# The experts' Gelu in half pieces, each followed by an exponential that nobody reads

## The chip, the cores and the metric

The kernel runs on one core of a Trainium2 chip. The metric is the device time of one execution in microseconds (us). A core has five engines that run side by side, each through its own queue in order: TensorE (PE, with its weight loads as PEld), VectorE (DVE), ScalarE (ACT), GpSimd (POOL) and SyncE (SP), which here only issues DMA transfers.

## The reference

The input is x, 4 sequences of 2048 tokens of 512 columns. Everything is in 32-bit floats.

```
xn  = layernorm(x)
qkv = xn @ qkv_w.T + qkv_b                      # 16 heads of 32 columns
att = softmax(q k^T * 32**-0.5) v               # per sequence and head, 2048 x 2048
a   = att @ proj_w.T + proj_b
idx = top_2(xn[:, 0, :] @ Wr + br)              # 2 of 8 experts for each sequence
h   = gelu(xn @ W1[idx] + b1[idx])              # the exact Gelu, 512 columns
f   = sum over the two experts of (h @ W2[idx] + b2[idx]) / 2
out = x + a + f
```

## The kernel before

**Units.** The work of attention is cut into 1024 units. A unit U is one sequence (4), one group of four heads (4), one chunk of 512 queries (4) and one tile of 128 keys (16 per chunk). For a unit, PE forms four score tiles of 128 keys x 512 queries (`shift`, line 725, writes minus the row maxima into the bank; `score`, line 733, adds the scores), and ACT takes their exponentials into one buffer `p` (line 849, four instructions of 512 columns). In the same turn of the loop PE forms four score tiles the other way round for a unit 22 turns ahead (`score_max`, line 715), whose maxima DVE takes (line 855). In each even unit, PE multiplies the last two `p` buffers with v (`weigh`, line 745, tile `acc`), and DVE adds that to a running sum. POOL adds the `p` buffers of a chunk up, one per unit (line 766; the last of a chunk is added by a DMA that POOL issues, line 764). There are four `p` buffers.

All PE results go to a ring of eight banks of 512 columns (`bank`, tag "bank"): each new tile takes the bank that was used longest ago, and has to wait until what was in it has been read. An even unit takes four banks for scores, four for the maxima's scores, and a ninth tile, `acc`.

**Dense products.** The other matrix products (q, k and v, the experts' two layers, the output projection) are laid into the odd units, one item each: 16 matmuls per item, most of them, which take PE 3.64 us. The class `Plan` decides which item goes into which odd unit. Some slots are fixed; the rest is filled in order. Every sixteenth slot (`s % NT == 5`) may be left empty, when the plan has slots to spare:

```python
if s in rests:
    owed += share
    if owed > 0 and not curve:
        owed -= 1
        continue
```

`curve` (line 147) keeps a slot from being left empty when the item just before it makes an activation due in it.

**The experts' layers.** The first layer (`w1` items) handles two chunks of 512 tokens at a time for one expert. It uses a scheme of seven half-size products (numbers 1 to 7 of `GAPS`) instead of eight, which `combine` adds up, on DVE, in two buffers `hT[0]` and `hT[1]`, one per chunk of tokens, each 128 x 4 column tiles x 512. A product comes in two halves q = 0, 1; half q fills the column tiles 2q and 2q+1. The eight items of one such block are, in order: 1 (q = 0), 1 (q = 1), 6, 7, 5 and 3 (q = 0), 5 and 3 (q = 1), 4, 2. So `hT[1]` has its first two column tiles after (3, 0), all four after (3, 1), and `hT[0]` is complete after (2, 1). There are 16 blocks (4 sequences, 2 pairs of chunks, 2 experts), and so 32 buffers to activate. After them come the second layer's items (`w2`), four for `hT[1]` (odd chunk) and then four for `hT[0]`.

**The activation.** `dense` puts a finished buffer under the number of a later unit, the next odd one:

```python
if (i, q) in ((3, 1), (2, 1)):
    at = U + 2 if U > 0 or U == -1 else U + 1
    curves[at] = hT[i == 3]
```

and the main loop issues the Gelu in that unit, right behind its four exponentials (lines 849 to 853). ACT computes a function from a table; where the next function isn't in the loaded table, the compiled program has an ACT_TABLE_LOAD ahead of it. The trace shows one ahead of each Gelu and one ahead of the first exponential after it. Other instructions on ACT that may stand between them are a normalisation of a token tile (`normal`, line 441), a copy (lines 524, 784), and three times a Sqrt (`root`, line 434).

The order on every engine is that in which the program issues (a manual schedule); waits between engines are derived from what each instruction reads and writes.

Of the kernel before, what the change touches and what calls it, by code (L numbers as in the profile page):

```python
# [9 lines left out]
F32 = mybir.dt.float32  # L10
BF16 = mybir.dt.bfloat16
U32 = mybir.dt.uint32
AF = mybir.ActivationFunctionType
# [4 lines left out]
P = 128  # L18
# [19 lines left out]
class Plan:  # L38
# [6 lines left out]
    def __init__(self, B, DC, NCH, NT, TPC):  # L45
# [13 lines left out]
        for G in range(1, B * DC):  # L59
            b, g = divmod(G, DC)  # L60
            first = (G - 1) * self.per_group
            for n, products in enumerate(GAPS):
                at = (11, 12, 13, 14, 15, 16, 17, 19) if g else (5, 6, 7, 8, 9, 11, 12, 13)
                fixed[first + 2 * at[n] + 1] = ("qk", b, g, products)
            if g == 0:
                at = [n for n in range(14, 32) if n % 8 != 2]
# [10 lines left out]
        for b in range(1, B):  # L77
            q1 = (b - 1) * self.per_seq + self.per_group
            q2 = q1 + self.per_group
            for k in range(TOP_K):  # L80
                at = q1 + ((NT - 1, q2 - q1 + 5 * NT - 1) if b > 1 else (-1, NT - 1))[k]
# [4 lines left out]
            for n in range(NT):  # L86
                self.extra.setdefault(q1 + 2 * (16 + n) + 1, []).append(("stats", b, n))
                c, i = divmod(n, TPC)
                at = q2 + 2 * (1 + 18 * (c // 2) + 5 * (c % 2) + i) + 1
# [3 lines left out]
            for p in range(NCH // 2):  # L93
                at = q2 + 2 * NT * (p + 1) - 1
# [46 lines left out]
        current, before, owed = [], None, 0  # L141
        for s in slots:
            if s in fixed:
                self.items[s] = [fixed.pop(s)]
                before = None
                continue
            curve = before is not None and before[0] == "w1" and before[4][-1] in ((3, 1), (2, 1))
            before = None
            if s in rests:
                owed += share  # L150
# [3 lines that stand above are left out]
            if not current:  # L154
                for queue in (proj, ffn):
                    if queue and queue[0][0] <= s:
                        current = queue.pop(0)[1]
                        break
            if current:
                before = current.pop(0)  # L160
                self.items[s] = [before]
# [77 lines left out]
def block_kernel(  # L239
# [16 lines left out]
    nc = tc.nc  # L256
# [12 lines left out]
    const = ctx.enter_context(tc.tile_pool(name="const", bufs=1))  # L269
# [7 lines left out]
    def bank(name):  # L277
        return ps.tile([P, CH], F32, tag="bank", name=name)
# [106 lines left out]
    nc.vector.tensor_copy(ident_b, ident)  # L385
    ones = const.tile([P, HD], F32, name="ones")
    nc.gpsimd.memset(ones, 1.0)
    ones_b = const.tile([P, P], BF16, name="ones_b")
    nc.gpsimd.memset(ones_b, 1.0)

# [90 lines left out]
    def product(pp, terms, last=True, first=True):  # L481

        for n, (lhsT, rhs) in enumerate(terms):
            for j in range(GH):
                nc.tensor.matmul(  # L485
                    pp[rows_of(j), :], lhsT[:, rows_of(j)], rhs,
                    start=(first and n == 0), stop=(last and n == len(terms) - 1),
                )

    kT, qT = {}, {}  # L490
    hT, bias, b1s = {}, {}, {}
# [16 lines left out]
    def project_v(b, n, xn, w, U):  # L508

        c, i = divmod(n, TPC)  # L510
        pp = bank(f"vps_{b}_{n}")
        product(pp, [(xn[:, d, ts(i, P)], w[:, d, :]) for d in range(DC)])
        t = pair.tile([P, D], F32, tag="vrow", name=f"v_{b}_{n}")
        nc.vector.tensor_tensor(t, pp, bv_bc, ALU.add)
        later(U + 2, lambda: nc.sync.dma_start(v_dram[b, c][:, i, :], t))

    def combine(i, x, c, b1, b2, on_dve):

        add = nc.vector.tensor_tensor
        biased = nc.vector.scalar_tensor_tensor  # L520
        if i == 1 and on_dve:
            nc.vector.tensor_copy(c[0, 0], x)
        elif i == 1:
            nc.scalar.activation(c[0, 0], x, AF.Identity)  # L524
        elif i == 6:
            add(c[0, 1], x, c[0, 0], ALU.add)
        elif i == 7:
            add(c[1, 0], x, c[0, 1], ALU.add)
        elif i == 5:
            biased(c[1, 1], x, b2, c[1, 0], ALU.add, ALU.add)  # L530
            add(c[0, 1], x, c[0, 1], ALU.add)
        else:
            at, b_ = {3: ((0, 1), b1), 4: ((1, 0), b2), 2: ((0, 0), b1)}[i]
            biased(c[at], x, b_, c[at], ALU.add, ALU.add)
# [29 lines left out]
    def blocks(kind, b, n, U):  # L564
# [10 lines left out]
        else:  # L575
# [4 lines left out]
            if n == 3:  # L580
                later(U + (2 if b == 0 else 4), lambda: nc.sync.dma_start(ws_dram[b, k], raw))

    outs = {}

    def dense(item, U, on_dve, between):
        kind, b = item[:2]
        tiles = [held[n] for n in plan.needs(item)]
        if kind == "qk":
            g, products = item[2:]
            for n, (i, p) in enumerate(products):  # L590
                wt, xt = tiles[2 * n : 2 * n + 2]
                pp = bank(f"qkps_{b}_{g}_{i}_{p}")
                product(pp, [(wt[:, d, 0, :], xt[:, d, :]) for d in range(2)])
                o = outs.setdefault((b, g, p), {})
                where = {1: (0, 0), 6: (0, 1), 7: (1, 0), 5: (1, 1)}.get(i)
                if where is not None:
                    c = 2 * p + where[1]
                    t = "kq"[where[0]]
                    o[where] = (kT if t == "k" else qT)[b, g, c] = kv_pool.tile(
                        [P, CH], F32, tag=t, name=f"{t}T_{b}_{g}_{c}",  # L600
                        bufs=2 * NCH if t == "k" else NCH + 3,
                    )
                combine(i, pp, o, bqkv[:, DC + g : DC + g + 1], bqkv[:, g : g + 1], on_dve)
                if n == 0:
                    between()
        elif kind == "v":
            n = item[2]
            project_v(b, n, tiles[1] if b else stage[0, n // TPC], tiles[0], U)
        elif kind == "w1":
            p, k, products = item[2:]  # L610
            for n, (i, q) in enumerate(products):
                wt, xt = tiles[2 * n : 2 * n + 2]
                if (i, q) in ((1, 0), (6, 0)):
                    cc = int(i == 6)
                    hT[cc] = stream.tile(
                        [P, DC, CH], F32, tag="h", name=f"h_{b}_{p}_{k}_{cc}", bufs=2
                    )
                pp = bank(f"hps_{b}_{p}_{k}_{i}_{q}")
                product(pp, [(wt[:, d, q, :], xt[:, d, :]) for d in range(2)])
                o = {(r, cc): hT[cc][:, 2 * q + r, :] for r in range(2) for cc in hT}  # L620
                cols = [b1s[b, k][:, 2 * q + r : 2 * q + r + 1] for r in range(2)]
                combine(i, pp, o, *cols, on_dve)
                if n == 0:
                    between()
                if (i, q) in ((3, 1), (2, 1)):
                    at = U + 2 if U > 0 or U == -1 else U + 1
                    curves[at] = hT[i == 3]
        elif kind == "w2":
            p, c, k, i = item[2:]
            w, row = tiles  # L630
            pp = bank(f"ops_{b}_{c}_{k}_{i}")
            product(pp, [(hT[c % 2][:, f, ts(i, P)], w[:, f, :]) for f in range(DC)])
            nc.vector.scalar_tensor_tensor(row, pp, 0.5, row, ALU.mult, ALU.add)  # L633
            later(U + 2, lambda: nc.sync.dma_start(part_dram[b, c, i], row))
        else:
            qc, i = item[2:]
            at, w, row = tiles
            pp = bank(f"prps_{b}_{qc}_{i}")
            product(pp, [(at[:, g, ts(i, P)], w[:, g, :]) for g in range(DC)])
            finish(b, qc, i, pp, row, U)  # L640

    def finish(b, qc, i, pp, row, U):
        tok = qc * CH + i * P
        nc.vector.tensor_tensor(row, pp, row, ALU.add)  # L644
        later(U + 2, lambda: nc.sync.dma_start(out[b, tok : tok + P, :], row))
# [15 lines left out]
    def sum_bias(t, other, pb):  # L661
        nc.gpsimd.tensor_tensor(t, t, other, ALU.add)
        nc.gpsimd.tensor_scalar(t, t, 0.5, None, ALU.mult)
        nc.gpsimd.tensor_tensor(t, t, pb, ALU.add)


    mv, sd, nb = stat_tiles(0)
# [27 lines left out]
    def place(u):  # L695
        rest, kt = divmod(u, NT)
        rest, qc = divmod(rest, NCH)
        return (*divmod(rest, DC), qc, kt)

    mx, negm, sacc, psums, sums, pT = {}, {}, {}, {}, {}, {}  # L700
    curves, waiting, ends = {}, {}, []

    def later(u, do):
        waiting.setdefault(u, []).append(do)
# [124 lines left out]
    for U in range(-LEAD, plan.units):  # L829
# [20 lines left out]
        curve = curves.pop(U, None)  # L850
        if curve is not None:
            flat = curve.rearrange("p f n -> p (f n)")
            nc.scalar.activation(flat, flat, AF.Gelu)
        for dst, t in maxima:
            nc.vector.tensor_reduce(dst, t, AX.X, ALU.max, negate=True)  # L855
        last = U + LEAD
# [7 lines left out]
        before = place(U - NT)[:3] if U >= NT else None  # L864
# [30 lines left out]
        for step, sb, n in plan.extra.get(U, []):  # L895
# [10 lines left out]
            else:  # L906
                c, i = divmod(n, TPC)
# [36 lines left out]
    U = plan.units  # L944
# [18 lines left out]
    for i in range(TPC):  # L963
        q = ts(i, P)
# [52 lines left out]
```

## Time and profile before

| | |
|---|---|
| median of 3 runs | 5042.79 us (5037.69 to 5044.59) |
| the profiled execution | 5042.55 us |
| its span, first to last instruction | 5040.8 us |
| mean granted TensorE clock | 0.997 |
| PE busy | 4947.0 us, 98% |
| POOL busy | 4429.2 us, 88% |
| DVE busy | 3740.2 us, 74% |
| ACT busy | 2394.0 us, 47% |
| ACT_TABLE_LOAD | 71, of 1.283 us each |
| Gelu, 128 x 2048 | 32, of 1.912 us each |

How to read the profile's rows: a group has its line, engine and operation, what it writes and reads with the shapes, how often; then the busy time in us and the mean of one in ns; then the idle time of the engine just before these instructions and what ended most of it. In a row of time the first two numbers are start and duration in us, and the brackets hold the idle time before and what ended it. "A <- B: 37.0, 35, 1.6" says that A waited for B 37.0 us in total, 35 times, 1.6 us at the longest.

### The profile page before, as it was taken

Reading aid. Unit: us, or ns where it says so; the run is one execution under the profiler, and the core shown is the slowest. Engines: PE = TensorE matmul, PEld = TensorE weight load, DVE = VectorE, ACT = ScalarE, POOL = GpSimd, SP = SyncE. Lnnn points to the kernel's source line nnn. Section 1 sums busy time; section 2 is a strip of 40 time slices with the busy share of each in tenths; the row PEclk is TensorE's granted clock in tenths of the full one; section 3 lists DMA queues with packets and bytes.
Section 4 is the critical chain, followed back from the end, with each engine's and each line's share of the span. In section 5 each row is a group of like instructions: output and inputs, shape, how many; then the busy total and the mean of one; then the engine's idle time right before and its main releaser. Section 6 shows DMA issues by size and latency. Waiting matters only on the chain. (4 is left out here: it accounts for less than half of the span.)

```text
span 5040.8 us, 107883 instructions
## 1 busy us (share of the span) xinstructions
PE 4947.0 (98%) x45028; PEld 1725.8 (34%) x45028; DVE 3740.2 (74%) x5909; ACT 2394.0 (47%) x4406; POOL 4429.2 (88%) x1498
## 2 busy tenths in 40 slices
PE   8999999999999999999999999999999999999998
PEld 2333333333333333333333333333333333333332
DVE  5777887777777788777777777877777777777762
ACT  1445445454444545454444444555444445454453
POOL 2799998999898998999889998999988988999981
PEclk9999999999999999999999999999999999999999
DMA  6333334433233434434224234434423343323312
GB/s 219 111 103 117 115 96 127 142 122 109 80 107 104 126 107 122 140 114 141 89 86 125 85 121 118 146 122 136 134 70 106 100 123 101 101 80 101 107 62 95
DMA packets 297128, 568.16 MB, mean 113 GB/s; under 512 B 24636, under 2 KB 144188, under 8 KB 279744
## 3 DMA queue, kind: packets, MB, share of 16 engines
q1 hardware_dynamic: 287568, 495.19, 29.4%
q0 software_dynamic: 9072, 66.06, 6.7%
q8 instruction: 354, 5.80, 0.5%
q14 instruction: 134, 1.10, 0.1%
HBM read 367.44 MB, written 127.66 MB: 98 GB/s over the span
## 5 line engine op out<-in xcount | busy, mean ns | idle before, releaser
L766 POOL TENSOR_TENSOR psum<-psum,p 128x2048 f32<-128x2048 f32 x819 | 3722.4, 4545 | 167.6 <-ACT p L849 129.2
L849 ACT ACTIVATE p<-s 128x512 f32<-128x512 f32 x4096 | 2118.0, 603 | 2364.9 <-PE m L715 2181.8
L855 DVE TENSOR_REDUCE mx<-m 128x1 f32<-128x512 f32 x4096 | 2544.2, 684 | 570.1 <-PE m L715 569.8
L733 PE MATMUL s<-qT,kT 32*128 32x512 f32 x8192 | 1919.1, 588 | 0.0
L715 PE MATMUL m<-kT,qT 32*128 32x512 f32 x8192 | 1911.3, 590 | 6.4 <-ACT h L524 3.4
L715 PEld LDWEIGHTS m<-kT,qT 32*128 32x128 f32 x8192 | 920.9, 184 | 334.9 <-issue 244.7
L745 PE MATMUL acc<-p,v 128*32 128x512 f32 x8192 | 988.5, 600 | 37.0 <-ACT p L849 37.0
L733 PEld LDWEIGHTS s<-qT,kT 32*128 32x128 f32 x8192 | 768.6, 185 | 29.2 <-issue 7.3
L485 PE MATMUL ops<-wb_w,h 128*32 128x512 f32 x4096 | 466.0, 595 | 0.6 <-ACT p L849 0.2
L745 PEld LDWEIGHTS acc<-p,v 128*32 128x32 f32 x8192 | 214.2, 109 | 737.0 <-ACT p L849 420.5
L762 POOL TENSOR_TENSOR psum<-p,p 128x2048 f32<-128x2048 f32 x63 | 287.5, 4563 | 203.2 <-ACT p L849 203.2
L754 DVE TENSOR_TENSOR sacc<-acc,sacc 128x512 f32<-128x512 f32 x448 | 309.9, 692 | 158.3 <-PE acc L745 158.3
L485 PE MATMUL hps<-xt,wt_w 128*32 128x512 f32 x3584 | 411.0, 596 | 2.5 <-ACT p L849 2.0
L725 PE MATMUL s<-negm,ones_b 32*128 32x512 bf16 x4096 | 405.7, 385 | 6.2 <-ACT p L849 5.9
L485 PE MATMUL qkps<-xt,wt_qk 128*32 128x512 f32 x3360 | 387.8, 599 | 9.8 <-ACT p L849 9.2
L725 PEld LDWEIGHTS <-ones_b 32*128 32x128 bf16 x4096 | 103.2, 91 | 858.2 <-issue 858.1
L870 DVE RECIPROCAL sums<-sums 128x128 f32<-128x128 f32 x252 | 237.6, 943 | 0.7 <-ACT sums L784 0.7
L485 PEld LDWEIGHTS ops<-wb_w,h 128*32 128x32 f32 x4096 | 120.0, 109 | 308.6 <-issue 229.8
L633 DVE SCALAR_TENSOR_TENSOR row<-ops,row 128x512 f32<-128x512 f32 x128 | 88.4, 691 | 170.3 <-PE ops L485 116.3
L485 PE MATMUL prps<-wb_proj,xl_at 128*32 128x512 f32 x1792 | 203.9, 595 | 0.3
L485 PEld LDWEIGHTS hps<-xt,wt_w 128*32 128x32 f32 x3584 | 103.3, 109 | 268.2 <-issue 186.1
L485 PEld LDWEIGHTS qkps<-xt,wt_qk 128*32 128x32 f32 x3360 | 97.3, 110 | 273.9 <-issue 181.6
(123 smaller groups left out, 1981.6 us busy)
## 6 DMA issues: line engine op xcount, KB each, us to landing
xt<-t_dram SPq DMA_DIRECT2D x181, 512.0 KB, 4.3
xt<-xn_dram SPq DMA_DIRECT2D x133, 512.0 KB, 5.0
psum<-p POOLq DMA_DIRECT2D x63, 1024.0 KB, 8.2
part_dram<-row SPq DMA_DIRECT2D x128, 256.0 KB, 2.0
v_dram<-v SPq DMA_DIRECT2D x64, 256.0 KB, 2.7
wt_w<-ws_dram SPq DMA_DIRECT2D x128, 128.0 KB, 3.3
v<-v_dram SPq DMA_DIRECT2D x64, 256.0 KB, 4.9
row<-in_x_dram SPq DMA_DIRECT2D x64, 256.0 KB, 6.5
```

Of the source, the lines that this page charges most:

```text
L485: nc.tensor.matmul(pp[rows_of(j), :], lhsT[:, rows_of(j)], rhs, start=(first and n == 0), stop=(last and n == len(terms) - 1),)
L633: nc.vector.scalar_tensor_tensor(row, pp, 0.5, row, ALU.mult, ALU.add)
L715: nc.tensor.matmul(t, qT[b, g, qc][r, ts(i, P)], kT[b, g, kc][r, :], start=True, stop=True)
L725: nc.tensor.matmul(tiles[j], ones_b[r, :], negm[b, g, qc][r, :], start=True, stop=False)
L733: nc.tensor.matmul(tiles[j], kT[b, g, kt // TPC][r, ts(kt % TPC, P)], qT[b, g, qc][r, :], start=False, stop=True,)
L745: nc.tensor.matmul(acc[r, :], held["v", (b, g, kt // TPC)][:, (kt + n) % TPC, r], pT[u + n][:, j, :], start=(n == 0), stop=(n == 1),)
L754: nc.vector.tensor_tensor(t, acc, t, ALU.add)
L762: nc.gpsimd.tensor_tensor(psums[b, g, qc], pT[u - 1], pT[u], ALU.add)
L766: nc.gpsimd.tensor_tensor(psums[b, g, qc], psums[b, g, qc], pT[u], ALU.add)
L849: nc.scalar.activation(pT[U][:, j, :], tiles[j], AF.Exp, scale=SCALE)
L855: nc.vector.tensor_reduce(dst, t, AX.X, ALU.max, negate=True)
L870: nc.vector.reciprocal(sums[before][:, q], sums[before][:, q])
```

## The change

The Gelu is done on two column tiles (128 x 1024) at a time. For `hT[1]` the two pieces follow the items with (3, 0) and (3, 1); for `hT[0]` both follow (2, 1), in the next odd unit and in the one after that. Directly behind each piece ACT computes an exponential of one column of a constant, into a tile that nothing reads. The plan's condition for a slot that must not be left empty is extended to the new units: after the item with (3, 0), and after the first `w2` item of an odd chunk.

```diff
@@ class Plan
-            curve = before is not None and before[0] == "w1" and before[4][-1] in ((3, 1), (2, 1))
+            curve = before is not None and (
+                before[0] == "w1" and before[4][-1] in ((3, 0), (3, 1), (2, 1))
+                or before[0] == "w2" and before[3] % 2 == 1 and before[5] == 0
+            )
@@ constants
+    unused = const.tile([P, 1], F32, name="unused")
@@ helpers
+    def following(U):
+
+        return U + 2 if U >= -1 else U + 1
...
+    def back_to_exp():
+
+        nc.scalar.activation(unused, ones[:, :1], AF.Exp)
@@ def dense, w1
-                if (i, q) in ((3, 1), (2, 1)):
-                    at = U + 2 if U > 0 or U == -1 else U + 1
-                    curves[at] = hT[i == 3]
+                if i == 3:
+                    curves[following(U)] = hT[1][:, 2 * q : 2 * q + 2, :]
+                if (i, q) == (2, 1):
+                    curves[following(U)] = hT[0][:, :2, :]
+                    curves[following(following(U))] = hT[0][:, 2:, :]
@@ main loop
         if curve is not None:
             flat = curve.rearrange("p f n -> p (f n)")
             nc.scalar.activation(flat, flat, AF.Gelu)
+            back_to_exp()
```

## The prediction

> **What bounds the kernel now.** I read first the page's shares of busy time, then who kept TensorE (PE) waiting, then ScalarE's (ACT's) groups by shape, then the order of time around one Gelu on ACT and on PE.
>
> ```profile
> PE 4947.0 (98%) x45028; PEld 1725.8 (34%) x45028; DVE 3740.2 (74%) x5909; ACT 2394.0 (47%) x4406; POOL 4429.2 (88%) x1498
> ```
>
> PE is busy 98% of the span of 5040.8 us, so only 94 us of PE idle can be won. ACT has half its time free; POOL (GpSimd) at 88% is the next limit. The waits of PE, longest first (total us, times, longest):
>
> ```profile
> PE acc L745 <- ACT p L849: 37.0, 35, 1.6
> PE qkps L485 <- ACT p L849: 9.2, 5, 4.7
> PE xt L455 <- ACT x L441: 6.0, 1, 6.0
> ```
>
> The first row is the only large one. In the order of time 31 of those waits, nearly all of 1.16 us, follow a Gelu directly. ACT's groups by shape:
>
> ```profile
> L849 ACT ACTIVATE p<-s 128x512 f32<-128x512 f32 x4096 | 2118.0, 603 | 2364.9 <-PE m L715 2181.8 <-issue 74.2 <-PE s L733 60.8
> L853 ACT ACTIVATE h<-h 128x2048 f32<-128x2048 f32 x32 | 61.2, 1912 | 0.4
> L849 ACT ACT_TABLE_LOAD x35 | 44.9, 1283 | 25.6 <-PE m L715 25.5
> L853 ACT ACT_TABLE_LOAD x32 | 41.1, 1283 | 0.6
> L441 ACT ACTIVATE xl_normal<-xl_normal,nb,sd 128x512 f32<-128x512 f32 x48 | 39.8, 829 | 0.0
> L434 ACT ACTIVATE sd<-sd 128x16 f32<-128x16 f32 x3 | 0.6, 215 | 7.5 <-DVE sd L433 7.5
> ```
>
> The load ahead of a Gelu starts at once (0.6 us idle over 32). The load back to Exp sits behind the wait of the next exponential: before its 35 instances ACT was idle 25.6 us, for scores (PE m). So 1.283 us of load starts only when the scores are ready. One Gelu on ACT in order of time (start, duration):
>
> ```profile
> 1718.64 2.07 ACT L849 ACTIVATE p<-s 128x512 f32<-128x512 f32 x4 [2.09 <-PE m L715]
> 1720.72 1.28 ACT L853 ACT_TABLE_LOAD   x1
> 1722.02 1.91 ACT L853 ACTIVATE h<-h 128x2048 f32<-128x2048 f32 x1
> 1724.24 1.28 ACT L849 ACT_TABLE_LOAD   x1 [0.31 <-PE m L715]
> 1725.53 2.07 ACT L849 ACTIVATE p<-s 128x512 f32<-128x512 f32 x4
> ```
>
> And PE beside it:
>
> ```profile
> 1718.82 0.59 PE L733 MATMUL s<-qT,kT 32*128 32x512 f32 x2
> 1719.34 3.64 PE L485 MATMUL hps<-xt,wt_w 128*32 128x512 f32 x32
> ...
> 1724.43 0.59 PE L733 MATMUL s<-qT,kT 32*128 32x512 f32 x2
> 1726.18 1.92 PE L745 MATMUL acc<-p,v 128*32 128x512 f32 x16 [1.16 <-ACT p L849]
> ```
>
> Undisturbed, PE goes on 0.52 us after the start of its last score matmul; here it took 1.75. That is **1.23 us lost** for a load that made the exponentials 1.28 late; so PE has 0.05 us of slack. The reason is in the code: in an even unit `acc` is the ninth tile of a ring of eight banks, so it takes the bank of the first score tile, which the first exponential frees.
>
> **What the losses before add up to.** I took, for all 32 Gelus, the time from the end of the four exponentials ahead to the start of those behind (4.82 here), and to the point where the scores were ready (3.53 here). 30 lose about 1.23: 36.9. One, at 2210 us, also has a 0.80 us normalisation (L441) on ACT between, with nothing extra on PE: 1.64. One, at 1980 us, also has the Sqrt with its own load, and the exponentials come at 6.22 instead of 3.53: 2.64. Sum **41.2 us**.
>
> **The change, part by part.** (1) *Half Gelus.* The two ACT rows of 512 and 2048 columns give (1912-603)/1536 = 0.852 ns a column, so 1024 columns are 603+436 = 1.04 us, or with the overhead taken from the 0.21 us of the tiny Sqrt 1.06. I take 1.05: 64 of them are 67 us of ACT instead of 61. (2) *64 more loads and 64 one-column exponentials.* The dummy has no wait: its operand is a constant, its target is nobody's. So its load starts when the half Gelu ends. The dummy takes 0.21, the row of the tiny Sqrt (0.215). Loads before: 32+35+4 = 71. After: 64+64+4+4 = 136. (3) *The chain in one piece.* From the end of the exponentials: 0.02 + load 1.283 + 0.015 + Gelu 1.05 + 0.02 + load 1.283 + 0.015 puts the dummy's start at 3.69. Adjacent exponentials overlap by 0.12 (four of 0.603 in 2.07), so the next real one can start between 3.78 and 3.90. I take 3.80, nearer the row of adjacent exponentials. Scores are ready at 3.53: late 0.27, less the slack of 0.05: **0.22 us lost a piece**, bounds 0.15 and 0.35. (For an undivided Gelu with the dummy the same sum is 4.65, late 1.12: nearly all of the 1.28 would stay. The halves are what makes the eager load fit.)
>
> (4) *Where the 64 pieces fall.* By the plan's rule every piece sits in an odd unit with a dense product of 3.64 us on PE: the product hides 3.53 us of ACT. Without a product, exponentials come 3.9 us apart and the window is 1.83; the price would be 2 us. The planner's new condition keeps the empty slots off these units: working the slots through by hand, three (units 53, 661, 901) move sixteen units on, and the products between move up. Same work, hence 0, with 2 us either way for what collides. Of the 64 pieces 45 meet nothing else: 45 x 0.22 = 9.9. Nine have PE transposes in their unit (of the maxima, or of a token tile), which widen the window to about 3.97: 0. Nine share the unit with a normalisation, which adds 0.80-0.10: chain 4.50, against scores ready at 4.13 (five, as the rows below show), 3.97 (two) and 3.53 (two): 5 x 0.32 + 2 x 0.48 + 2 x 0.92 = 4.4. One meets the Sqrt: 6.22-0.86+1.283+0.25 = 6.89, lost 3.3. Sum after: **17.6**.
>
> ```profile
> 847.55 1.28 ACT L853 ACT_TABLE_LOAD   x1
> 848.85 1.91 ACT L853 ACTIVATE h<-h 128x2048 f32<-128x2048 f32 x1
> 850.66 0.80 ACT L441 ACTIVATE xl_normal<-xl_normal,nb,sd 128x512 f32<-128x512 f32 x1
> 851.66 1.28 ACT L849 ACT_TABLE_LOAD   x1 [0.19 <-PE m L715]
> ```
>
> The load waited here until 4.13 us after the exponentials' end (847.53).
>
> (5) *New dependences.* The piece of `hT[1]` column tiles 0 and 1 runs while VectorE (DVE) writes tiles 2 and 3 of the same buffer. If waits were kept by whole buffers, DVE would wait for the piece. The trace speaks against it: key matmuls on the first columns of `wkq` start at 18.17 us, while the DMA into its other columns, issued at 8.20, took 12.7 us to land. So 0; by whole buffers DVE's three additions (2.2 us) would start when the piece ends, 4.4 us into a unit of 5.6, and the next maxima come 1 us late in 16 units: 16 us. No DMA is added or moved but for the three shifted slots, and the first W2 product still follows its pieces by one unit or more. On ACT only the next exponentials, a normalisation or the Sqrt queue behind the dummy, all counted above.
>
> (6) *POOL.* A gain on PE stays only if POOL follows. POOL waits for exponentials again soon after almost every Gelu, so its train moves up too. The exception is the stretch from 1006.9 to 1156 us, where POOL never waits and PE is then held 0.97 us for it (`qkps` at 1160): the pair of Gelus in it gives 2 x 1.23 - 4 x 0.22 = 1.6, lost again. Bounds 0 and 6.
>
> Sum: 41.2 - 17.6 - 1.6 = 22.0. Span 5040.8 - 22.0 = 5018.8; the profiled execution took 5042.55 in all, 1.75 around its span, and the median of the runs is 0.24 above it: **5021 us**, 0.43% faster.
>
> [...]
>
> **The rivals.** *All hidden*: if the overlap at the dummy is larger or the half Gelu shorter by 0.25 us, plain pieces lose nothing: 41.2-7.7-1.6 = 32 us, 5011; were the normalisations hidden as well, 5006. Against: no row shows a shorter chain. Chance 0.13. *POOL becomes the bound*: more stretches like 1006 to 1156, with PE's gain returned as waits for p buffers; at 88% busy, and with trains of six to eight adds between waits, half the gain could go: 5032, all of it 5043. For: PE's waits of 0.35 to 4.73 behind POOL at 929, 1160, 3051 and 3446. Against: POOL waited 195 times for exponentials. Chance 0.10. *The load stays with the next real exponential* (the slower end): if the dummy were dropped or its load placed behind the wait, each of 64 pieces would cost 1.23 where 32 did: 32 x 1.23 = 39 more, 5082. It decides as soon as a piece loses over 41.2/64 = 0.64, a chain 0.42 longer than mine; any queueing of that size around the dummy does the same. Against: loads ahead of Gelu and Sqrt start at once. Chance 0.07. The rest, 0.70, is the forecast.
>
> **How the numbers follow.** By its bounds of 0.15 to 0.35 for 45 plain pieces (6.8 to 15.8), POOL's 0 to 6 and 2 either way, the likeliest case runs from 5014 to 5034. The range of 5007 to 5035 adds most of the all-hidden case and leaves out the worse half of POOL's and the slower one. Runs before spread over 7 us, so 0.2% (10 us) is about what can be told from no change: faster by that 0.85, within it 0.08, slower 0.07.
>
> **What would show it.** Right: 136 loads, those back to Exp on the dummy's line with no idle before them; PE's wait of `acc` for p from 37 us in 35 to some 12 us in about 60, each 0.1 to 0.3; ACT busy near 2497; half Gelus of 1.05. Wrong: loads still on the exponentials' line; waits of over 0.64 each; Gelus in units without a product; or PE's waits gone and POOL's rows wider.

## The result, and the profile after

The changed kernel takes 5022.76 us (median of 6, 5019.70 to 5027.52) against 5040.08 before (6 runs): a ratio of 0.9966, 95% interval 0.9953 to 0.9979. It is 17 us faster, where 22 were forecast. (The base had been put at 5042.79, the median of three runs; over six it is 5040.08.) The profiled execution took 5027.02 us with a span of 5025.2, 15.6 us less than the span before; it is one of the slower of the six.

The page, first lines:

```profile
span 5025.2 us, 108029 instructions
...
PE 4955.8 (99%) x45028; PEld 1727.3 (34%) x45028; DVE 3738.9 (74%) x5909; ACT 2491.2 (50%) x4567; POOL 4430.7 (88%) x1498
```

ACT is busy 97 us longer: 65 more loads take 83.4 us, the dummies 13.0 and the half Gelus 6.5 more than the whole ones did; some 6 us of that overlap with the exponentials behind. ACT's groups by shape, those that the change touches:

```profile
L867 ACT ACT_TABLE_LOAD x64 | 82.1, 1283 | 1.1
L678 ACT ACT_TABLE_LOAD x64 | 82.1, 1283 | 0.9
L867 ACT ACTIVATE h<-h 128x1024 f32<-128x1024 f32 x64 | 67.7, 1058 | 0.7
L678 ACT ACTIVATE unused<-ones 128x1 f32<-128x1 f32 x64 | 13.0, 203 | 0.7
L863 ACT ACT_TABLE_LOAD x4 | 5.1, 1283 | 14.9 <-PE m L729 14.8
```

The load back to Exp has moved from the exponentials' line to the dummy's (L678), with 0.9 us of idle before 64 of them. One piece in order of time on ACT, the same Gelu as shown before:

```profile
1715.24 2.07 ACT L863 ACTIVATE p<-s 128x512 f32<-128x512 f32 x4 [1.89 <-PE m L729]
1717.32 1.28 ACT L867 ACT_TABLE_LOAD   x1
1718.62 1.06 ACT L867 ACTIVATE h<-h 128x1024 f32<-128x1024 f32 x1
1719.69 1.28 ACT L678 ACT_TABLE_LOAD   x1
1720.99 0.20 ACT L678 ACTIVATE unused<-ones 128x1 f32<-128x1 f32 x1
1721.10 2.04 ACT L863 ACTIVATE p<-s 128x512 f32<-128x512 f32 x4
```

From the end of the exponentials (1717.31) to the next it is 3.79 us; 3.80 was worked out. And on PE:

```profile
1721.04 0.59 PE L747 MATMUL s<-qT,kT 32*128 32x512 f32 x2
1721.73 1.92 PE L759 MATMUL acc<-p,v 128*32 128x512 f32 x16
```

Start to start 0.69 us, where 0.52 is undisturbed and 1.75 was needed before: 0.17 lost. Measured in this way over all pieces, **the Gelus' units lose 16.6 us instead of 41.3**, a gain of 24.7. This puts the gain a little too low: in six of the 64 units (2.5 us of the 16.6) the distance was just as long before, without a Gelu, because PE has other work in between. The largest, before and after:

```profile
1952.06 0.59 PE L733 MATMUL s<-qT,kT 32*128 32x512 f32 x2
1953.36 1.92 PE L745 MATMUL acc<-p,v 128*32 128x512 f32 x16
```

```profile
1946.97 0.59 PE L747 MATMUL s<-qT,kT 32*128 32x512 f32 x2
1948.27 1.92 PE L759 MATMUL acc<-p,v 128*32 128x512 f32 x16
```

So the pieces lose about 14 us, and the Gelus' units gain about 27. PE's waits:

```profile
PE qkps L489 <- ACT p L863: 15.0, 9, 5.5
PE s L739 <- ACT p L863: 6.0, 2, 5.0
PE acc L759 <- ACT p L863: 4.1, 12, 0.8
```

The wait of `acc` is nearly gone (37.0 before), but that of `qkps` has grown from 9.2 to 15.0. So some of this gain is given back elsewhere. PE at 1155 us, the place where the prediction put a loss of 1.6:

```profile
1150.73 0.59 PE L747 MATMUL s<-qT,kT 32*128 32x512 f32 x2
1155.18 5.30 PE L489 MATMUL qkps<-xt,wt_qk 128*32 128x512 f32 x32 [3.87 <-ACT p L863]
```

The exponentials that it waits for are held by a `p` buffer:

```profile
1154.54 2.06 ACT L863 ACTIVATE p<-s 128x512 f32<-128x512 f32 x4 [5.82 <-DMA psum<-p]
```

That DMA is issued by POOL, at the end of a train of additions:

```profile
1144.82 0.87 POOL L778 DMA_DIRECT2D psum<-p  x1 [0.30 <-POOL psum L780]
```

The wait was 0.97 us before. And the product behind it takes 5.30 us instead of 3.64. The granted clock tells why; time by stretches of the same part of the work, after (the columns are the stretch and its length, busy time by engine with counts, the clock, DMA):

```profile
1140.00:1170.00 30.00, 26.13 (x228) 9.06 (x224) 18.88 (x30) 12.12 (x24) 24.95 (x7) 0.94 0.61 178
```

and before:

```profile
1150.00:1180.00 30.00, 29.03 (x268) 10.18 (x264) 22.98 (x37) 14.03 (x28) 27.46 (x8) 1.00 0.62 186
```

The clock is at half for 3.41 us right after the wait (0.50 from 1155.16 to 1158.57). In the two profiled executions such stretches, leaving out the one at the very end, add up to 20.5 us in four places before and to 37.5 us in eight places after. PE is busy in nearly all of that time (17.9 and 34.9 us), at half speed, so half of the difference, 8.5 us, is lost. PE's idle time outside the Gelus' units grew too, from 48.2 to 52.9 us, of which 2.9 are the wait at 1155. The account of the two executions is then: 27.2 gained at the Gelus, less 8.5 of half clock, less 4.7 of idle time, leaves 14.0, against 15.6 measured; 1.6 us are not placed.

Set side by side by the start of each unit's first exponential, the two traces gain in the chunks that hold Gelus and give back mainly in three: 4.5 us in the chunk that began at 1145 us before, 3.0 in that from 1973 us (the Sqrt), 2.0 in that from 3430 us. All three have one of the new stretches at half clock. The first is all wait and clock: 3.87 - 0.97 = 2.9 us of wait more, and 5.30 - 3.64 = 1.7 us of a slower product. Not every new stretch stands at a longer wait: at 3045 us PE waits 2.19 us where it waited 2.47 before, without half clock (see the last section). (Two other chunks, where an empty slot has moved, give 2.3 and 2.2 us and get more than that back in the next.)

### The profile page after: what moved, and what is told of

Read it like the earlier page. It is cut to its first block, busy times and chain, and to the rows that moved or that the text cites. A ratio compares the mean times of both kernels' runs of the same rounds, so it can differ in the third digit from the quotient of the medians.

```text
span 5025.2 us, 108029 instructions
## 1 busy us (share of the span) xinstructions
PE 4955.8 (99%) x45028; PEld 1727.3 (34%) x45028; DVE 3738.9 (74%) x5909; ACT 2491.2 (50%) x4567; POOL 4430.7 (88%) x1498
```

## The experiments

**The dummy alone, behind whole Gelus** (the kernel before with this):

```diff
             nc.scalar.activation(flat, flat, AF.Gelu)
+            nc.scalar.activation(unused, ones[:, :1], AF.Exp)
```

> The kernel before, with the exponential of a constant behind each undivided Gelu; nothing else. Theory (the load must fit into the time in which a dense product hides ScalarE): load, Gelu of 1.91, load and dummy take 4.65 us to the next exponentials instead of 4.82, against scores at 3.53, so a plain Gelu still loses about 1.07 instead of 1.23; only the four that share their unit with PE transposes gain more (0.6). Sum of the gain about 6 us: 5034 (5030 to 5038). Rival (the eager load alone is what counts, the halves are incidental): the load is hidden, about 25 us gained, 5015.

Measured: 5039.98 us, ratio 0.9999 (0.9991 to 1.0007): no change. ACT in order of time:

```profile
1718.65 1.28 ACT L854 ACT_TABLE_LOAD   x1
1719.94 1.91 ACT L854 ACTIVATE h<-h 128x2048 f32<-128x2048 f32 x1
1721.86 1.28 ACT L855 ACT_TABLE_LOAD   x1
1723.15 0.20 ACT L855 ACTIVATE unused<-ones 128x1 f32<-128x1 f32 x1
1723.26 2.04 ACT L850 ACTIVATE p<-s 128x512 f32<-128x512 f32 x4
```

The load starts at once, but the chain is 4.62 us long (1718.64 to 1723.26). The Gelus' units lose 36.1 us instead of 41.3. Of these 5 us, 4 show between the two profiled executions (5036.9 against 5040.8) but nothing that can be told in the medians; the forecast of 5034 was a miss by 6. The rival's 25 us are out: an eager load without the halves gains nothing that can be measured.

**The halves alone** (the changed kernel without the dummy):

```diff
             nc.scalar.activation(flat, flat, AF.Gelu)
-            back_to_exp()
```

> The changed kernel without the exponential of a constant: half Gelus in 64 units. Theory: the load back to Exp sits behind the wait for scores again, 64 times instead of 32, 1.23 us each: about 79 us lost instead of 41, so 5078 (5070 to 5084), slower than before by 38. Rival (what gains is that ScalarE's work is spread into smaller pieces or the slots are moved): faster than before, 5020 to 5035.

Measured: 5078.49 us, ratio 1.0075 (1.0062 to 1.0089). The groups on ACT and PE's wait:

```profile
L863 ACT ACT_TABLE_LOAD x67 | 86.0, 1283 | 90.6 <-PE m L729 88.7 <-issue 1.8
```

```profile
PE acc L759 <- ACT p L863: 71.4, 66, 1.4
```

The loads wait for scores again, and the units lose 80.3 us: 62 of the 64 lose 1.22 or 1.23. The halves need the dummy as much as the dummy needs the halves. This is also the prediction's slower rival, made real: it said 39 us more.

**The plan alone** (the kernel before with the new condition for empty slots):

```diff
-            curve = before is not None and before[0] == "w1" and before[4][-1] in ((3, 1), (2, 1))
+            curve = before is not None and (
+                before[0] == "w1" and before[4][-1] in ((3, 0), (3, 1), (2, 1))
+                or before[0] == "w2" and before[3] % 2 == 1 and before[5] == 0
+            )
```

> The kernel before with the plan's new condition alone: three empty slots (units 53, 661, 901) move sixteen units on, Gelus undivided, no dummy. Theory: no change, 5040, within 3 us. Rival (the moved slots take POOL's pressure off and make part of the gain): 5 us or more faster.

Measured: 5043.93 us, ratio 1.0005 (0.9996 to 1.0013): no change that can be told. The moved slots bring nothing of the gain.

**A longer chain** (the changed kernel with a dummy of 512 columns):

```diff
-    unused = const.tile([P, 1], F32, name="unused")
+    unused = const.tile([P, CH], F32, name="unused")
...
-        nc.scalar.activation(unused, ones[:, :1], AF.Exp)
+        nc.scalar.activation(unused, bv_bc, AF.Exp)
```

> The changed kernel with a dummy of 512 columns (of the v bias, constant too) instead of one: 0.60 us instead of 0.20, so the chain to the next exponentials is 4.2 instead of 3.79 and a plain piece loses 0.58 instead of 0.17; with 10 pieces beside a normalisation at 0.6 to 1.2 and one beside the Sqrt at 3.5 about 40 us are lost, as many as before the change. Theory: the gain is gone, 5039 (5034 to 5044). Rival (the loss does not follow the chain's length; what counts is that the load starts early): 5023 to 5028.

Measured: 5042.08 us, ratio 1.0003 (0.9995 to 1.0011).

```profile
1712.34 1.28 ACT L678 ACT_TABLE_LOAD   x1
1713.63 0.63 ACT L678 ACTIVATE unused<-bv_bc 128x512 f32<-128x512 f32 x1
1714.17 2.04 ACT L863 ACTIVATE p<-s 128x512 f32<-128x512 f32 x4
```

```profile
1714.80 1.92 PE L759 MATMUL acc<-p,v 128*32 128x512 f32 x16 [0.26 <-ACT p L863]
```

The exponentials come 0.43 us later behind the dummy's load than in the changed kernel, and most pieces lose 0.59 or 0.60. The sum over the units is 40.4 us, as many as before the change, and the gain is gone. So the loss follows the length of the chain, and the prediction's break-even (0.42 longer) stands where it was put.

**A shorter chain** (the changed kernel with thirds instead of halves, 96 pieces):

```diff
-                if i == 3:
-                    curves[following(U)] = hT[1][:, 2 * q : 2 * q + 2, :]
...
+                cut = (0, 683, 1366, 2048)
+                if i == 3:
+                    flat = hT[1].rearrange("p f n -> p (f n)")
+                    curves[following(U)] = flat[:, cut[q] : cut[q + 1]]
+                    if q == 1:
+                        curves[following(following(U))] = flat[:, cut[2] :]
```

(`hT[0]` likewise in three odd units, and the plan's condition covers the new units.)

> The changed kernel with each buffer's Gelu in three pieces of 683, 683 and 682 columns, each followed by the dummy, 96 pieces in 96 units with a dense product. Theory: the chain is shorter by 341 columns or 0.29 us, 3.50 from the exponentials' end to the next, under the 3.53 at which scores are ready: plain pieces lose nothing, those with a normalisation 0.05 to 0.6, the one with the Sqrt 2.8; about 5 us lost instead of 16.6. If all of it comes through 5011; with a third of it lost to POOL and to a lower PE clock after waits, 5015 (5009 to 5019). Rival (each switch has a price of its own that the chain doesn't show): 32 more pairs of loads make it slower than the changed kernel, 5025 to 5040.

Measured: 5017.32 us, ratio 0.9953 (0.9939 to 0.9966).

```profile
1702.85 1.28 ACT L872 ACT_TABLE_LOAD   x1
1704.14 0.78 ACT L872 ACTIVATE h<-h 128x683 f32<-128x683 f32 x1
1704.92 1.28 ACT L684 ACT_TABLE_LOAD   x1
1706.22 0.20 ACT L684 ACTIVATE unused<-ones 128x1 f32<-128x1 f32 x1
1706.38 2.06 ACT L869 ACTIVATE p<-s 128x512 f32<-128x512 f32 x4
```

The exponentials start 3.55 us after the last ones ended, their undisturbed distance, and 80 of the 96 pieces lose nothing. The rival, a price of each switch that the chain doesn't show, is out: 32 more pairs of loads made nothing slower. What is left is 10.9 us: 2.85 beside the Sqrt and twice 1.61, where the third piece fell in a unit with half a dense product. A unit without any product, which the prediction priced at 2 us, got no piece and was not measured.

**POOL relieved, in both kernels.** To see whether what is given back is lost behind POOL, its 64 additions of the summed output biases to the token rows were left out, first from the kernel before, then from the changed one. Both outputs lack those biases.

```diff
         for t, key in row_ready.pop(U, []):
-            nc.gpsimd.tensor_tensor(t, t, bias[key[0]], ALU.add)
+            pass
```

> The kernel before without POOL's 64 additions of the summed output biases to the token rows (1.31 us each, 84 us of POOL); those biases are missing from its output. It is the base for the next run. Theory: only PE's waits that come from a late POOL go (the one at 1160 us and some of the others, with the stretches at half clock that follow them): 5034 (5028 to 5040).

> The changed kernel with the same 64 additions left out, its output lacking the same biases. Theory (of the 24.7 us that the Gelus' units gain, some 8 are lost where POOL is the limit, through PE's wait of 3.9 us at 1155 and the half clock after such waits): with POOL relieved the wait at 1155 is gone and the gain over the run above is 21 to 25 us, so 5011. Rival (the missing 8 us are lost for another reason, DVE or DMA, or lie in the units of the Gelus): the gain stays at 16 to 18, and PE's wait at 1155 is there still.

Measured: 5036.99 and 5008.81 us, ratios to the kernel before 0.9992 (0.9983 to 1.0000) and 0.9940 (0.9926 to 0.9953). The same change gains 28.2 us here instead of 17. The stretch around the former wait, in the changed kernel without the additions:

```profile
1130.00:1160.00 30.00, 30.00 (x284) 10.82 (x276) 22.54 (x36) 13.37 (x27) 27.04 (x8) 1.00 0.70 202
```

PE is busy throughout and the clock is full. The Gelus' units lose 41.3 and 16.6 us, the same as with the additions; half clock fell from 23.9 to 17.1 us, worth 3.4 more. 24.7 and 3.4 make 28.1, but that they meet the medians so closely is luck: the profiled executions differ by 30.1 us, 2.4 of it ahead of the first unit, where the clock became full at 17.1 us instead of 23.0. The rival is out: the gain in the Gelus' units did not change, and what was missing came back with POOL relieved, through the wait at 1155 and less half clock. Other waits behind POOL stayed, such as 5.86 us at 2357. That the gain came out above the forecast of 21 to 25 is the half clock, which the forecast had left even, and the 2.5 us by which the Gelus' gain is put too low.

**The additions on DVE, with the thirds:**

```diff
-            nc.gpsimd.tensor_tensor(t, t, bias[key[0]], ALU.add)
+            nc.vector.tensor_tensor(t, t, bias[key[0]], ALU.add)
```

> The kernel with thirds, and the 64 additions of the summed biases on VectorE instead of POOL: 84 us less on POOL, 64 x 0.69 = 44 us more on DVE, which is 74% busy. Theory: PE's waits behind POOL (15.6 us on qkps) shrink to about 5, fewer stretches at half clock: 5007 (5000 to 5014). Rival (DVE's maxima come later by 0.7 us and hold banks of the ring): 5017 or more.

Measured: 5166.77 us, ratio 1.0244 (1.0230 to 1.0258), a clear miss.

```profile
L901 DVE TENSOR_TENSOR row<-row,bias 128x512 f32<-128x512 f32 x64 | 178.5, 2789 | 0.0
```

```profile
PE m L735 <- DVE row L649: 28.9, 18, 2.3
```

An addition took 2.79 us on average, from 0.63 to 4.87, not 0.69. My 0.69 was from additions that read one operand from PSUM (322 of the 448 of `sacc` ran wholly inside an addition of POOL's in the changed kernel, and none took longer than 0.69); here both are in SBUF. PE then waits for DVE, and the clock is at half for 109 us. The trace shows why they are long:

```profile
236.51 4.52 POOL L782 TENSOR_TENSOR psum<-p,p 128x2048 f32<-128x2048 f32 x1 [6.49 <-ACT p L869]
236.78 4.80 DVE L901 TENSOR_TENSOR row<-row,bias 128x512 f32<-128x512 f32 x1
```

DVE's addition starts inside one of POOL's and ends 0.55 us after it (241.58 and 241.03). So it is with 62 of the 64: they end 0.55 us behind POOL's instruction.

**Thirds, kept clear** of the two units with half a product and of the unit with the Sqrt, and beside it the changed kernel once more:

```diff
     def following(U):

-        return U + 2 if U >= -1 else U + 1
+        U = U + 2 if U >= -1 else U + 1
+        short = any(it[0] == "qk" and len(it[-1]) == 1 for it in plan.items[U])
+        if short or any(e[0] == "root" for e in plan.extra.get(U, [])):
+            return following(U)
+        return U
```

(The plan's condition covers one more unit than in the first version with thirds.)

> The kernel with thirds, its pieces kept out of the two units with a half dense product (qk with one product, where a piece lost 1.61 us) and out of the unit with the Sqrt (2.85). Theory: some 8 us lost in 96 units instead of 10.9 with the Sqrt's own load still there: 5 us less at the Gelus than the thirds' first version at best, so 5013 (5009 to 5018), below the changed kernel of the same job by 6 to 12. Rival (what is won at the Gelus is lost again to PE waits behind POOL and half clock): as the changed kernel, within 4 us.

> The changed kernel once more, unaltered, beside the run above on the same chip: 5023 (5018 to 5028).

Measured: 5019.52 us, ratio 0.9954 (0.9941 to 0.9968), and 5024.74, ratio 0.9964 (0.9951 to 0.9978). The 96 pieces now lose 4.9 us, 11.7 less than the changed kernel's, and 5 us show; the intervals of the two overlap, and the forecast of 5013 was a miss. PE waits 5.12 us at 1150, longer than ever, and the time at half clock is 34.1 us against 37.5. So the Gelus are all but free, and over half of what is won there beyond the halves does not show. Part of it is PE's waits of `qkps` for exponentials, 17.2 us against 14.1 in the changed kernel beside it; the rest was not traced. The thirds are the fastest complete version found by their medians, not by their intervals.

## Why the prediction was right

The range held, the sign was right, and the chain that the forecast rests on was measured to 0.01 us. That 5021 came so close to 5022.76 is partly luck: the gain was 4.7 us short of the forecast, and the base was 2.7 us below the median of three runs that the forecast started from.

*What bounds before.* 41.2 us lost at 32 Gelus was the reading; start to start in the trace gives 41.3.

*The chain of a piece.* 3.80 us was the sum, 3.79 is measured. The half Gelu was put at 1.05 (1.058), the dummy at 0.21 (0.203). A plain piece was put at 0.22 lost, and 0.17 is measured, inside the bounds.

*The sum after.* 17.6 was forecast; 16.6 is measured, and about 14 without the six units whose distance was as long before. One count was off: ten pieces stand beside a normalisation, not nine. The Sqrt's unit lost 3.1, not 3.3.

*The dependences and the moved slots* cost nothing, as said: DVE's additions did not wait for the pieces, and the plan alone changed nothing that can be told (+2.5 us, with an interval that holds 1).

*Step (6), POOL, was mis-sized.* The place was right, the train of additions from 1007 us to the wait at 1155. Its price was put at 1.6 us, the pair's own gain; the wait grew by 2.9 and the chunk gave back 4.5. It was also not the only place: the wait of 4.73 us, which the prediction counts among those at 929, 1160, 3051 and 3446, lies at 2373, and it grew by 0.8. The term that was missing is PE's clock: behind the wait of 3.87 us at 1155 it was at 0.50 for 3.41 us, and the product there took 1.7 us longer. Over the profiled execution 17.0 us more at half clock than before made 8.5 us. The two together, less what the pieces came out cheaper, are why 17 us came instead of 22; POOL's bounds of 0 to 6 were too narrow, as they had no half clock in them.

*What would show it.* 136 loads, the idle on the dummy's line and ACT's 2491 us (2497 said) came as described. The waits of `acc` did not: 12 waits of 4.1 us in all, not some 60 of 12 us, because the last score matmul's 0.59 us reach 0.07 past the undisturbed start of `acc` (0.52), and of a delay of 0.17 only 0.10 us is then idle, which is not listed as a wait. It shows from start to start.

*More switches* were no loss by themselves: the number of table loads went from 71 to 136 (and to 200 with the thirds) and the time fell (ratios 0.9966 and 0.9953); what counted here was whether a load lies in time that PE's work covers.

## What to carry to other kernels

A table load that the compiler puts behind the next instruction's wait can be pulled ahead of it by a tiny instruction of the same function that waits for nothing (here the idle time before the loads back to Exp went from 25.6 us to 0.9 on the dummy's line). Here it paid only where load, work, load and dummy nearly fitted into the 3.53 us that PE's product covers: a chain of 4.62 us gained nothing that could be measured, one of 3.79 gained 17 us, and at 3.55 80 of 96 pieces lost nothing. So cut the work until it fits. Work out that time for the unit where each piece falls, and check the units with less cover one by one. And where TensorE is the bound, look at the granted clock behind its waits. Here the wait of 3.87 us cost twice: once for itself, and 1.7 us in the 3.41 us at half clock behind it.

## What the runs showed of the hardware

*The stretches at half clock lasted 3.413 or 6.827 us.* So it is, leaving out the first 30 us and the end, with the four before the change and the eight after it, and each lies at a PE wait. In each of the twelve profiles, every change of the clock comes a whole number of 3.4133 us after the clock first became full, to 0.02 us; windows are counted from there in what follows. Before the change it became full at 22.69 us (16 transposes on PE took 3.68 us ahead of that and 1.97 behind it), and half clock began at 766.79, 2371.06, 3207.32 and 4944.71: 218, 688, 933 and 1442 such windows later.

What followed a wait went with PE's idle time inside one window. Before and after the change, the 11 windows at full clock with over 2.0 us of idle time, from 2.05 (the window from 3042.73 us after) to 3.41 (from 1151.75 us after), were all followed by half clock, 3 of the 7 with 1.46 to 1.84 us, and none with less. In the eleven profiles other than that with the additions on DVE, each of the 47 windows at full clock with over 2.0 us of idle time was followed by half clock, 11 of the 33 with 1.43 to 2.0 us, and none with less. (With the additions on DVE, one with 0.96 and one with 1.29 us were.) So the wait of 2.47 us at 3051 before the change, which fell into two windows, cost no clock, and that of 2.19 at 3045 after it, nearly all in one, did. Before and after, the window of the wait and the next (behind the stretch and its length stands PE's busy time; the clock is third from the end):

```profile
3046.91:3050.32 3.41, 2.02 (x20) 0.84 (x17) 2.83 (x5) 0.00 (x0) 3.41 (x1) 1.00 0.84 258
3050.32:3053.74 3.42, 2.34 (x24) 0.81 (x28) 1.48 (x4) 2.07 (x4) 1.22 (x2) 1.00 0.42 141
```

```profile
3042.73:3046.14 3.41, 1.35 (x16) 0.46 (x20) 2.38 (x5) 2.00 (x4) 1.70 (x1) 1.00 0.79 280
3046.14:3049.56 3.42, 3.42 (x24) 0.74 (x16) 0.75 (x1) 0.06 (x1) 3.21 (x1) 0.50 0.38 108
```

The clock first became full between 16.1 and 23.0 us in the twelve profiles (22.69 before the change, 21.93 after it), so the windows did not lie at the same times in them. Still, the changed kernel had a mean clock of 0.995 to 0.996 in all its 11 runs, and the kernel before 0.996 to 0.998. A single wait of 1.46 us was enough for half clock at 3198 us after the change (1.00 in the window of the wait, 0.50 in the next, from 3199.74 to 3203.16).

*A table load cost 1.283 us, and next to nothing around it.* Before and after the change each of the 71 and 136 loads lasts 1283 ns. Those that wait for no data (all 32 and 64 ahead of Gelus, and all 64 ahead of the dummies) start at most 0.02 us after the instruction before them ends, and the next instruction starts 0.01 us after the load.

*The DVE additions with both operands in SBUF ended behind the POOL instruction that was running.* In the run with the additions on DVE they took up to 4.87 us, and 62 of 64 ended 0.55 us after the end of the POOL instruction during which they had started.
